# Half of a graph layer's rows turned by VectorE through DRAM, in a hand-made order, on one core

## Chip, cores, metric

The kernel runs on one core of one Trainium2 chip. The metric is the device time of one execution in microseconds (us). A ratio is the mean time of one kernel's fast runs over the mean of the other's in the same rounds on the same chip, so it is not quite the ratio of the medians quoted beside it. The profile shows one execution of each kernel.

## The reference

4096 nodes of 512 features go through two layers, each with a layer norm, a relu and a residual:

```python
h = relu(layernorm(x));  x = x + L0(h, adj, ptr, Wq, bq, Wk, bk, Wv, bv)   # attention in 32 graphs of 128 nodes
h = relu(layernorm(x));  x = x + L1(h, adj, W, a_origin, a_dst)            # graph attention, 8 heads of 64

# L1, per head: mx = h @ W[head];  logits[i, j] = s_i + t_j
# attn = softmax over j of logits where adj > 0;  out = attn @ mx
```

In L1 the term s_i falls out of the softmax, so a row j needs only e_j = exp(t_j) for each head and the products e_j * mx_j. The kernel prepares these for 32 tiles ("rows" below) of 128 nodes, then multiplies each of 32 masks (adj > 0) with all of them. The change is in the preparation, here called the **row stage**.

## The kernel before

One row of layer 1 is normalised (VectorE and GpSimd), turned so that features lie on partitions (TensorE, with a relu on the way out of PSUM, the memory that its results land in), projected (TensorE), weighed by e (VectorE), and split into a rounded part (ScalarE) and a rest (GpSimd):

```python
def norm(src, hn):
    stats = small.tile([P, 6], F32, name="stats")
    nc.vector.bn_stats(stats, src)
    mv = small.tile([P, 2], F32, name="mv")
    nc.vector.bn_aggr(mv, stats)
    ...                                                    # rstd on GpSimd: add, then pow
    nc.vector.tensor_scalar(hn, src, mv[:, 0:1], rstd, ALU.subtract, ALU.mult)

def relu_T(ps_pool, hn, dst):
    pt = ps_pool.tile([P, KC, P], F32, name="pt")
    for k in range(KC):
        nc.tensor.transpose(pt[:, k, :], hn[:, ts(k, P)], ident)
    nc.scalar.activation(dst, pt, AF.Relu)

def prepare(i, hT, part):
    pm = project1(ps_p, hT, w1x)                           # 2 x 4 matmuls into two PSUM banks
    e = sb2.tile([P, EW], F32, name="e")
    nc.gpsimd.memset(e[:, EC:], 1.0)
    nc.scalar.activation(e[:, ES:EC], pm[1][:, HW : HW + H], AF.Exp)
    nc.gpsimd.tensor_copy(e_all[:, i, :], e[:, ES:EC])
    weigh(e, pm)                                           # two multiplications of 256 columns on VectorE
    split(e, part)
    parts.append(part)
...
for i in range(n - 1, NT):                                 # the row stage; a scheduler orders each engine
    hT = nhT
    if i + 1 < NT:
        nhT = normed1(i + 1)
    prepare(i, hT, part_tile(lo if i < LO else hi, i))
...
for i in range(NT - 1):                                    # the aggregation
    tot = aggregate(sb3, ps_g, i, lambda j: parts[j])      # begins with load_mask: load, turn, widen
```

## Time and profile before

| | before |
|---|---|
| device time, median of 6 runs | 966.8 us (965.0 to 967.74) |
| profiled execution | 962.86 us, span 961.1, clock 0.999 |
| row stage (last attention product of layer 0 starts, to first aggregation product) | 361.88 to 465.60: 103.7 us |
| after the row stage | 465.60 to 961.1: 495.5 us |

The prediction below reads the main lines. Two more are needed for the row stage: the first is the line of TensorE's timeline where the row stage begins (start, duration, engine, line, operation, destination and sources, shape, count). The second is a group of the view by line and shape between 345 and 470 us (busy us and mean ns, then idle time ahead of the group and who ended it).

```profile
361.88 1.02 PE L501 MATMUL pp<-v,sT 128*128 128x512 f32 x2
```

```profile
L127 PE MATMUL pt<-ident,row 128*128 128x128 f32 x99 | 15.2, 276 | 6.2 <-DVE row L121 6.1
```

Apart from the 1.17 us ahead of the aggregation, TensorE's idle time in this stage stands ahead of the turnings (L127), which wait for VectorE's normalisation (L121).

### The profile page before, as it was taken

Reading aid. Unit: us, or ns where it says so; the run is one execution under the profiler, and the core shown is the slowest. Engines: PE = TensorE matmul, PEld = TensorE weight load, DVE = VectorE, ACT = ScalarE, POOL = GpSimd, SP = SyncE. Lnnn points to the kernel's source line nnn. Section 1 sums busy time; section 2 is a strip of 40 time slices with the busy share of each in tenths; the row PEclk is TensorE's granted clock in tenths of the full one; section 3 lists DMA queues with packets and bytes.
Section 4 is the critical chain, followed back from the end, with each engine's and each line's share of the span. In section 5 each row is a group of like instructions: output and inputs, shape, how many; then the busy total and the mean of one; then the engine's idle time right before and its main releaser. Section 6 shows DMA issues by size and latency. Waiting matters only on the chain.

```text
span 961.1 us, 13194 instructions
## 1 busy us (share of the span) xinstructions
PE 937.3 (98%) x5051; PEld 817.2 (85%) x5051; DVE 460.7 (48%) x983; ACT 260.7 (27%) x507; POOL 185.0 (19%) x344
## 2 busy tenths in 40 slices
PE   8999999989999998899999999999999999999997
PEld 5676677766677776788899999999999999999997
DVE  4678777776766348655142332424233242423322
ACT  5766676666762222333100000000000000000000
POOL 2221213222122115555110101001010100101010
PEclk9999999999999999999999999999999999999999
DMA  9999889898884124222012213132231212122111
GB/s 347 419 349 389 314 324 368 351 369 343 343 335 158 34 87 122 77 66 55 1 54 80 85 49 88 49 83 54 79 82 50 88 50 83 52 80 81 51 45 35
DMA packets 58180, 148.22 MB, mean 154 GB/s; under 512 B 6402, under 2 KB 23170, under 8 KB 49922
## 3 DMA queue, kind: packets, MB, share of 16 engines
q1 hardware_dynamic: 48178, 130.31, 39.0%
q10 hardware_dynamic: 9936, 17.05, 4.7%
q8 instruction: 40, 0.66, 0.3%
q14 instruction: 26, 0.21, 0.1%
HBM read 113.77 MB, written 33.55 MB: 153 GB/s over the span
## 4 chain that ended last, share of the span: by engine, by line
PE 89%; DVE 4%; DMA 2%; POOL 2%; ACT 2%; issue 1%; SPq 0%; ACTq 0%; DVEq 0%; POOLq 0%
PE pg L284 50%; PE pp L428 11%; PE pp L416 10%; PE pp L243 9%; PE pp L501 3%; PE pss L474 3%; PE pt L127 2%; DMA row<-x_d 1%; PE pl L284 1%; POOL part L231 1%; DMA xg<-x 1%; DVE a L136 1%; DVE row L121 1%; ACT junk L451 1%; POOL rstd L120 0%
## 5 line engine op out<-in xcount | busy, mean ns | idle before, releaser
L284 PE MATMUL pg<-part,at 128*128 128x348 f32 x3008 | 479.6, 322 | 1.2 <-DVE e L252 1.2
L284 PEld LDWEIGHTS pg<-part,at 128*128 128x128 f32 x3008 | 479.1, 188 | 1.6 <-issue 1.5
L277 DVE CAST at<-at 128x4096 fp32r<-128x4096 fp8e4 x32 | 74.0, 2313 | 312.2 <-PE pg L284 312.2
L298 ACT COPY tot<-pg 128x522 f32<-128x522 f32 x31 | 18.5, 598 | 455.8 <-PE pg L284 455.8
L451 ACT ACTIVATE junk<-a 128x2048 bf16<-128x2048 f32 (+15 forms) x92 | 124.4, 1353 | 47.1 <-DVE x L503 25.0
L243 PE MATMUL pp<-w1x,hT 128*128 128x256 f32 (+1 forms) x512 | 117.3, 383 | 0.0
L428 PE MATMUL pp<-wv,hT 128*128 128x512 f32 x256 | 114.9, 592 | 0.0
L416 PE MATMUL pp<-hT,m_sb 128*128 128x256 f32 x512 | 113.2, 379 | 0.0
L416 PEld LDWEIGHTS pp<-hT,m_sb 128*128 128x128 f32 x512 | 96.2, 190 | 12.8 <-issue 0.5
L243 PEld LDWEIGHTS pp<-w1x,hT 128*128 128x128 f32 x512 | 94.9, 190 | 13.3
L428 PEld LDWEIGHTS pp<-wv,hT 128*128 128x128 f32 x256 | 48.6, 190 | 60.7 <-issue 60.7
L136 DVE TENSOR_SCALAR a<-a 128x512 fp8e4<-128x512 f32 x256 | 98.1, 460 | 1.8 <-DMA a_d<-a 1.8
L609 POOL COPY den_all<-tot 128x1 f32<-128x1 f32 x31 | 5.7, 184 | 369.2 <-DVE tot L299 369.2
L128 ACT ACTIVATE hT<-pt 128x512 f32<-128x512 f32 x64 | 36.9, 597 | 67.7 <-PE pt L127 67.6
L613 POOL TENSOR_TENSOR tot<-tot,row 128x512 f32<-128x512 f32 x31 | 39.9, 1288 | 61.8 <-DVE tot L304 61.8
L231 POOL TENSOR_TENSOR part<-e,part 128x522 fp32r<-128x522 f32 x32 | 42.2, 1318 | 43.1 <-ACT part L230 35.5
L118 POOL TENSOR_SCALAR ve<-mv 128x1 f32<-128x1 f32 x64 | 18.6, 294 | 150.9 <-DVE mv L116 150.8
L252 DVE TENSOR_TENSOR e<-pp,e 128x256 f32<-128x256 f32 x64 | 26.4, 415 | 29.3 <-ACT e L379 26.0
L270 DVE STREAM_TRANSPOSE at<-mw 128x1024 f32<-128x1024 f32 x32 | 39.6, 1236 | 0.0
L120 POOL TENSOR_TENSOR rstd<-ve,neghalf 128x1 f32<-128x1 f32 x64 | 38.4, 602 | 4.4
L432 DVE TENSOR_TENSOR v<-pp,bv_sb 128x512 f32<-128x512 f32 x32 | 22.0, 688 | 33.9 <-PE pp L428 33.9
L420 ACT ACTIVATE gT<-pp,c_sb 128x256 f32<-128x256 f32 x64 | 29.7, 467 | 28.7 <-PE pp L416 28.3
(101 smaller groups left out, 608.0 us busy)
## 6 DMA issues: line engine op xcount, KB each, us to landing
a<-adj SPq DMA_DIRECT2D x64, 1024.0 KB, 12.9
a_d<-a SPq DMA_DIRECT2D x32, 512.0 KB, 10.2
row<-x_d SPq DMA_DIRECT2D x64, 256.0 KB, 3.4
mw<-a_d SPq DMA_DIRECT2D x128, 128.0 KB, 4.0
xg<-x SPq DMA_DIRECT2D x16, 512.0 KB, 4.6
x_d<-x ACTq DMA_DIRECT2D x32, 256.0 KB, 4.2
out<-tot ACTq DMA_DIRECT2D x31, 256.0 KB, 3.8
wkT_sb<-wkT SPq DMA_DIRECT2D x4, 256.0 KB, 5.0
```

Of the source, the lines that this page charges most:

```text
L120: nc.gpsimd.tensor_tensor(rstd, ve, neghalf, ALU.pow)
L128: nc.scalar.activation(dst, pt, AF.Relu)
L136: nc.vector.tensor_scalar(a8v[:, u], av[:, u], 0.0, None, ALU.is_gt, saturate=False)
L231: nc.gpsimd.tensor_sub(dst[:, :, 1, :], e3, dst[:, :, 0, :].bitcast(F32))
L243: nc.tensor.matmul(pm[g][:, :n], hT[:, k, :], w1x[:, k, g * HW : g * HW + n], start=(k == 0), stop=(k == KC - 1),)
L270: nc.vector.transpose(at8.rearrange("p c n b -> p (c n b)").bitcast(F32).rearrange("p (c u n) -> p c u n", c=NW, n=B), mw.rearrange("p u ( ...
L277: nc.vector.tensor_copy(at.rearrange("p (c b) q -> p c b q", b=BY), at8.rearrange("p c q b -> p c b q"))
L284: nc.tensor.matmul(pg[:, : 2 * CW1], at[:, j, :], part(j)[:, c].rearrange("p s w -> p (s w)"), start=(j == 0), stop=(j == NT - 1),)
L416: nc.tensor.matmul(pp[:, : G * P], m_sb[:, k, ts(m, P)], hT[:, k, :], start=(k == 0), stop=(k == KC - 1),)
L428: nc.tensor.matmul(pp, hT[:, k, ts(t, P)], wv[:, k, :], start=(k == 0), stop=(k == KC - 1))
L451: nc.scalar.activation(junk[:, c0:c1], a[:, c0:c1], AF.Exp, scale=2.0 * NEG, accum_out=sums[:, n : n + 1],)
L613: nc.gpsimd.tensor_add(num, num, row)
```

## The change

The intent: take the turning of rows 16 to 31 off TensorE. VectorE turns blocks of 32x32 instead; four rows together ("a block", 1 MB) are written to DRAM and read back so that the right blocks come to the right partitions. The nodes of the four rows come out mixed, and the masks and the fallback path follow the mixed order. Because VectorE then has more to do, ScalarE weighs four of the eight heads for rows 8 to 15. VectorE, ScalarE, GpSimd and the load queue no longer follow the scheduler but the order of the program, and the first mask is loaded and converted within it; the second mask and the checks come after the rows. The core of the diff (the fallback and the mixed mask order are cut):

```diff
+MIXED = NT // 2          # rows 16 to 31 are turned by VectorE
+AHEAD = 8
...
-            n = len(ahead)
-            nhT = ahead[-1]
-            for i in range(n - 1, NT):
-                hT = nhT
-                if i + 1 < NT:
-                    nhT = normed1(i + 1)
-                prepare(i, hT, part_tile(lo if i < LO else hi, i))
+            def turn(i):
+                c, b = divmod(i, BY)
+                if b == 0:
+                    blocks[c] = sb4.tile([P, P // B, KC, BY, B], F32, name="blocks")
+                nc.vector.transpose(
+                    blocks[c][:, :, :, b], rows[i].rearrange("p (k q f) -> p q k f", k=KC, f=B)
+                )
+                if b == BY - 1:
+                    nc.sync.dma_start(hT_d[c], blocks[c].rearrange("p q k b r -> p q (k b r)"))
...
+                for i in range(n, NT):
+                    far, near = i + AHEAD, i + 2
+                    ...                                     # loads of rows
+                    if MIXED < far <= NT:
+                        turn(far - 1)
+                    if far % BY == 1 and MIXED + BY < far <= NT + 1:
+                        move(far // BY - 1)                 # four reads of a block from DRAM
+                    ...                                     # first mask: words, turn, widening
+                    low()                                   # GpSimd's rest of row i - 2
+                    if far < NT:
+                        of[far] = moments(rows[far])
+                    if near < MIXED:
+                        of[near] = moments(rows[near])
+                    ...                                     # TensorE turning of row i + 1 < 16
+                    pm = project1(ps_p, hTs[i], w1x)
+                    if before:
+                        low = finish(*before, later=True)   # weigh and copy row i - 1
+                    if near < MIXED:
+                        norm(rows[near], rows[near], of[near])
+                    if far < NT:
+                        norm(rows[far], rows[far], of[far])
+                    e = weights(i, pm)                      # exp
+                    halves = (1, 0)
+                    if i < MIXED:
+                        halves = (0,)
+                        for h in range(H // 2, H):
+                            nc.scalar.mul(...)              # ScalarE weighs four heads
+                    before = (e, pm, part_tile(lo if i < LO else hi, i), halves)
+                    if far < NT:
+                        nc.scalar.activation(rows[far], rows[far], AF.Relu)
```

More of the change, by code (lines that the diff above doesn't have):

```diff
@@ L84 @@
     a_d = dram.tile([NT, P, N // BY], F32, name="a_d")
+    hT_d = dram.tile([NW, P, P // B, KC * P], F32, name="hT_d")
     x1_d = dram.tile([NT, P, D], F32, name="x1_d")
@@ L108, in load_adj, with moments @@
         return a
-    def norm(src, hn):
+    def moments(src):
         stats = small.tile([P, 6], F32, name="stats")
@@ L120, in norm @@
         nc.gpsimd.tensor_tensor(rstd, ve, neghalf, ALU.pow)
-        nc.vector.tensor_scalar(hn, src, mv[:, 0:1], rstd, ALU.subtract, ALU.mult)
+        return mv[:, 0:1], rstd
+    def norm(src, hn, of=None):
+        mean, rstd = of or moments(src)
+        nc.vector.tensor_scalar(hn, src, mean, rstd, ALU.subtract, ALU.mult)
     def relu_T(ps_pool, hn, dst):
@@ L133, in mask_bytes @@
         a8v = a8.rearrange("p (u c q b) -> p u c b q", c=NW, q=B, b=BY)[:, :, half]
-        av = a.rearrange("p (c b u q) -> p u c b q", c=NW // 2, b=BY, q=B)
+        order = ("p (c b u q) -> p u c b q", "p (c u b q) -> p u c b q")[h]
+        av = a.rearrange(order, c=NW // 2, b=BY, q=B)
         for u in range(P // B):
@@ L225, in fold, with split, low @@
         return m_sb, c_sb, u_sb, z_sb
-    def split(e, dst):
+    def split(e, dst, later=False):
         e3 = e.rearrange("p (c w) -> p c w", c=CB)
         nc.scalar.copy(dst[:, :, 0, :], e3)
-        nc.gpsimd.tensor_sub(dst[:, :, 1, :], e3, dst[:, :, 0, :].bitcast(F32))
+        def low():
+            nc.gpsimd.tensor_sub(dst[:, :, 1, :], e3, dst[:, :, 0, :].bitcast(F32))
+        if later:
+            return low
+        low()
     def load_row(pool, i):
@@ L247, in project1, with weigh @@
         return pm
-    def weigh(e, pm):
-        for g in (1, 0):
+    def weigh(e, pm, halves=(1, 0)):
+        for g in halves:
             nc.vector.tensor_tensor(
@@ L257, in weigh, with load_words @@
             )
-    def load_mask(sb, i):
+    def load_words(sb, i):
         mw = sb.tile([P, P // B, N // BY // (P // B)], F32, name="mw", bufs=1)
-        for q in (0, 1, 2, 3):
+        for q in range(P // B):
             nc.sync.dma_start(
@@ L268, in load_mask, with turn_words @@
             )
+        return mw
+    def turn_words(sb, mw):
         at8 = sb.tile([P, NW, P, BY], FP8, name="at8", bufs=1)
@@ L275, in load_mask, with widen @@
         )
-        at = sb.tile([P, NT, P], F32R, name="at")
+        return at8
+    def widen(at, at8, c0=0, c1=NW):
         nc.vector.tensor_copy(
-            at.rearrange("p (c b) q -> p c b q", b=BY), at8.rearrange("p c q b -> p c b q")
-        )
+            at[:, c0 * BY : c1 * BY].rearrange("p (c b) q -> p c b q", b=BY),
+            at8[:, c0:c1].rearrange("p c q b -> p c b q"),
+        )
+    def load_mask(sb, i, at):
+        widen(at, turn_words(sb, load_words(sb, i)))
         return at
@@ L287, in product, with aggregate @@
         )
-    def aggregate(sb, ps_g, i, part):
-        at = load_mask(sb, i)
+    def aggregate(sb, ps_g, at, part):
         pg = ps_g.tile([P, CB, 512], F32, name="pg")
@@ L306, in graphs_are_tiles @@
     def graphs_are_tiles(sb):
-        ptr_i = sb.tile([1, NPTR], I32, name="ptr_i", bufs=1)
+        ptr_i = sb.tile([1, NPTR], I32, name="ptr_i", tag="row3", bufs=1)
         nc.sync.dma_start(ptr_i, ptr)
@@ L373, in normed1, with weights @@
                 return hT
-            def prepare(i, hT, part):
-                pm = project1(ps_p, hT, w1x)
+            def weights(i, pm):
                 e = sb2.tile([P, EW], F32, name="e")
@@ L380, in prepare, with finish @@
                 nc.gpsimd.tensor_copy(e_all[:, i, :], e[:, ES:EC])
-                weigh(e, pm)
-                split(e, part)
+                return e
+            def finish(e, pm, part, halves=(1, 0), later=False):
+                weigh(e, pm, halves)
                 parts.append(part)
+                return split(e, part, later)
+            def prepare(i, hT, part):
+                pm = project1(ps_p, hT, w1x)
+                finish(weights(i, pm), pm, part)
             with (
+                tc.tile_pool(name="adj0", bufs=AB, side="right") as ap,
                 tc.tile_pool(name="w0", bufs=1, side="right") as wp,
-                tc.tile_pool(name="adj0", bufs=AB, side="right") as ap,
                 tc.tile_pool(name="sb0", bufs=2, side="right") as sb,
@@ L574 @@
             )
-            n = len(ahead)
-            nhT = ahead[-1]
-            for i in range(n - 1, NT):
-                hT = nhT
-                if i + 1 < NT:
-                    nhT = normed1(i + 1)
-                prepare(i, hT, part_tile(lo if i < LO else hi, i))
+            sb5 = prep.enter_context(tc.tile_pool(name="sb5p", bufs=2, reuse_waits="tile"))
+            begun = ExitStack()
+            sb4 = begun.enter_context(
+                tc.tile_pool(name="sb4p", bufs=2, side="right", reuse_waits="tile")
+            )
@@ new lines, with load @@
+            rows, of, blocks, hTs = {}, {}, {}, {}
+            def load(i):
+                if i < NT:
+                    name, bufs = ("rowm", 5) if i >= MIXED else ("rown", 3)
+                    rows[i] = sb4.tile([P, D], F32, name=name, bufs=bufs)
+                    nc.sync.dma_start(rows[i], x1_d[i])
+            def turn(i):
[4 more added lines that the diff above has]
+                    blocks[c][:, :, :, b], rows[i].rearrange("p (k q f) -> p q k f", k=KC, f=B)
+                )
+                if b == BY - 1:
+                    nc.sync.dma_start(hT_d[c], blocks[c].rearrange("p q k b r -> p q (k b r)"))
@@ new lines, in move @@
+            def move(c):
+                hT = sb5.tile([P, P // B, KC, P], F32, name="hT4")
+                for q in range(P // B):
+                    nc.sync.dma_start(
+                        hT[ts(q, B)].rearrange("p u k m -> p u (k m)"),
+                        hT_d[c, :, q].rearrange("(u f) w -> f u w", f=B),
+                    )
+                for u in range(BY):
+                    hTs[c * BY + u] = hT[:, u]
+            E = mybir.EngineType
+            with tc.manual_schedule(engines={E.DVE, E.Activation, E.Pool, E.SP}):
+                n = len(ahead) - 1
+                hTs[n] = ahead[n]
+                before = None
+                for i in (1, 2):
+                    load(n + i)
+                for i in range(MIXED, n + AHEAD + 2):
+                    load(i)
+                norm(rows[n + 1], rows[n + 1])
+                low = lambda: None
+                for i in range(n, NT):
+                    far, near = i + AHEAD, i + 2
+                    if near + 1 < MIXED:
+                        load(near + 1)
+                    load(far + 2)
+                    if MIXED < far <= NT:
+                        turn(far - 1)
+                    if far % BY == 1 and MIXED + BY < far <= NT + 1:
+                        move(far // BY - 1)
+                    if far == NT + 1:
+                        begun.close()
+                        sb3a = straight.enter_context(
+                            tc.tile_pool(name="sb3a", bufs=1, side="right", reuse_waits="tile")
+                        )
+                        ata = sb3a.tile([P, NT, P], F32R, name="ata")
+                        words = load_words(sb3a, 0)
+                    if i == NT - 4:
+                        at8 = turn_words(sb3a, words)
+                    if i in (NT - 3, NT - 2):
+                        half = (i - NT + 3) * NW // 2
+                        widen(ata, at8, half, half + NW // 2)
+                    low()
+                    if far < NT:
+                        of[far] = moments(rows[far])
+                    if near < MIXED:
+                        of[near] = moments(rows[near])
+                    if i + 1 < MIXED:
+                        hTs[i + 1] = sb2.tile([P, KC, P], F32, name="hT1")
+                        relu_T(ps_t, rows[i + 1], hTs[i + 1])
+                    pm = project1(ps_p, hTs[i], w1x)
[10 more added lines that the diff above has]
+                        for h in range(H // 2, H):
+                            nc.scalar.mul(
+                                e[:, ts(h, HD)], pm[1][:, ts(h - H // 2, HD)],
+                                e[:, ES + h : ES + h + 1],
+                            )
+                    before = (e, pm, part_tile(lo if i < LO else hi, i), halves)
+                    if far < NT:
+                        nc.scalar.activation(rows[far], rows[far], AF.Relu)
+                low()
+                finish(*before)
@@ L590, with mask_of @@
         nc.gpsimd.memset(held, 1.0)
+        atb = sb3.tile([P, NT, P], F32R, name="atb", bufs=1)
+        def mask_of(i):
+            return ata if i == 0 else load_mask(sb3a, i, (ata, atb)[i % 2])
         def hold(n, src, bound, op):
@@ L607 @@
             nc.sync.dma_start(row, x1_d[i])
-            tot = aggregate(sb3, ps_g, i, lambda j: parts[j])
+            tot = aggregate(sb3, ps_g, mask_of(i), lambda j: parts[j])
             nc.gpsimd.tensor_copy(den_all[:, i : i + 1], tot[:, ES : ES + 1])
@@ L629 @@
         nc.sync.dma_start(row, x1_d[i])
-        at = load_mask(sb3, i)
+        at = mask_of(i)
         ps_l = straight.enter_context(tc.tile_pool(name="ps_l3", bufs=2, space=PSUM))
@@ L862, with level_rows @@
                     tc.tile_pool(name="ps_m4", bufs=2, space=PSUM) as ps_m,
-                    tc.For_i(0, NT, 1) as i,
                 ):
-                    hT = sb.tile([P, KC, P], F32, name="hT1")
-                    row = load_row(sb, i)
-                    norm(row, row)
-                    relu_T(ps_t, row, hT)
-                    pm = project1(ps_m, hT, w1x)
-                    te = small.tile([P, H], F32, name="te")
-                    nc.vector.tensor_tensor(te, pm[1][:, HW : HW + H], shift, ALU.subtract)
-                    nc.vector.tensor_scalar(te, te, 0.0, None, ALU.min)
-                    e = sb.tile([P, EW], F32, name="e")
-                    nc.gpsimd.memset(e[:, EC:], 1.0)
-                    nc.scalar.activation(e[:, ES:EC], te, AF.Exp)
-                    weigh(e, pm)
-                    split(e, parts_e[:, ds(i, 1)].rearrange("p o c s w -> p (o c) s w"))
+                    def level_rows(i, row):
+                        hT = sb.tile([P, KC, P], F32, name="hT1")
+                        norm(row, row)
+                        relu_T(ps_t, row, hT)
+                        pm = project1(ps_m, hT, w1x)
+                        te = small.tile([P, H], F32, name="te")
+                        nc.vector.tensor_tensor(te, pm[1][:, HW : HW + H], shift, ALU.subtract)
+                        nc.vector.tensor_scalar(te, te, 0.0, None, ALU.min)
+                        e = sb.tile([P, EW], F32, name="e")
+                        nc.gpsimd.memset(e[:, EC:], 1.0)
+                        nc.scalar.activation(e[:, ES:EC], te, AF.Exp)
+                        weigh(e, pm)
+                        split(e, parts_e[:, ds(i, 1)].rearrange("p o c s w -> p (o c) s w"))
+                    with tc.For_i(0, MIXED, 1) as i:
+                        level_rows(i, load_row(sb, i))
+                    with tc.For_i(MIXED, NT, BY) as i:
+                        for u in range(BY):
+                            row = sb.tile([P, D], F32, name="row1")
+                            for b in range(BY):
+                                nc.sync.dma_start(
+                                    row[ts(b, B)],
+                                    x1_d[ds(i + b, 1), ts(u, B)].rearrange("o p d -> (o p) d"),
+                                )
+                            level_rows(i + u, row)
                 with (
@@ L884 @@
                     nc.sync.dma_start(sofar, out[ds(i * P, P), :])
-                    tot = aggregate(sb, ps_g, i, lambda j: parts_e[:, j])
+                    at = load_mask(sb, i, sb.tile([P, NT, P], F32R, name="at"))
+                    tot = aggregate(sb, ps_g, at, lambda j: parts_e[:, j])
                     alone = small.tile([P, 1], F32, name="alone")
```

## The prediction

> **What bounds the kernel now.** I read the page first: busy shares, the forty slices, the chain that ended last.
>
> ```profile
> PE 937.3 (98%) x5051; PEld 817.2 (85%) x5051; DVE 460.7 (48%) x983; ACT 260.7 (27%) x507; POOL 185.0 (19%) x344
> ...
> PE 89%; DVE 4%; DMA 2%; POOL 2%; ACT 2%; issue 1%; SPq 0%; ACTq 0%; DVEq 0%; POOLq 0%
> ```
>
> TensorE is busy for 98% of the span and is 89% of the chain. So only two things can shorten the kernel: fewer TensorE instructions, or closing the gaps in which it waits. The change touches nothing before about 345 us (TensorE's order is the same in both programs up to layer 0's tail) and nothing but the mask buffers after about 465 us. So I split 345 to 470 us by stretches; the columns are length, then busy time and instruction count of each engine.
>
> ```profile
> 345.00:394.00 49.00, 42.83 (x207) 34.09 (x206) 36.27 (x81) 11.97 (x30) 21.81 (x40) 1.00 0.31 92
> 394.00:461.00 67.00, 67.00 (x341) 58.28 (x340) 36.60 (x82) 21.93 (x51) 37.88 (x83) 1.00 0.22 59
> 461.00:470.00 9.00, 7.83 (x44) 7.08 (x43) 2.57 (x7) 1.43 (x3) 2.60 (x3) 1.00 0.01 2
> ```
>
> From 394 to 461 us TensorE has no gap at all: layer 1's rows follow each other every 3.945 us (starts 398.07, 402.01, 405.96). Before that it idles 49.00 - 42.83 = 6.2 us, after it 1.2 us: 7.4 us together. The timeline of TensorE shows where:
>
> ```profile
> 376.88 0.66 PE L127 MATMUL pt<-ident,row 128*128 128x128 f32 x4 [3.02 <-DVE row L121]
> 385.76 0.66 PE L127 MATMUL pt<-ident,row 128*128 128x128 f32 x4 [1.20 <-DVE row L121]
> 393.63 0.66 PE L127 MATMUL pt<-ident,row 128*128 128x128 f32 x4 [1.54 <-DVE row L121]
> 465.60 4.70 PE L284 MATMUL pg<-part,at 128*128 128x348 f32 x28 [1.17 <-DVE e L252]
> ```
>
> A row's turning waits for VectorE's normalisation, because the scheduler had put two masks' conversions and the checks on ptr ahead of it on VectorE. In the chain, one row is "PE pt L127 x4" of 0.44 us (the turning) and "PE pp L243 x16" of 3.51 us (the projection).
>
> **What the Trainium skill says.**
> - "TensorE: Matmul & The Clock Gate", section "Architectural detail: the array is 16× 32×32, not 1× 128×128": ScalarE and VectorE are strict FIFO. The trace agrees: the 3.02 us gap above is a normalisation behind a 2.26 us mask conversion. This matters for a hand-made order: each wait in it stops all that stands behind.
> - "VectorE: DVE Perf Modes", section "The three transpose paths": VectorE turns 32x32 blocks only. That is why the change needs DRAM and mixed rows. The trace has the mask's turn, 1236 ns for 1024 elements a partition, so I estimate 0.65 us for 512.
> - "SBUF — State Buffer", section "Who interferes with whom": VectorE in a two-port mode and GpSimd exclude each other for a whole instruction. The trace agrees: the normalisation takes 0.55 us, but 1.44 us at 395.70, where GpSimd's 1.23 us subtraction had begun at 395.63.
> - "DMA: Bandwidth & Descriptors", section "Anatomy of one DMA — SWDGE (gpsimd) path": about 2 us are fixed. Here the path is another one; a 256 KB row load lands after 3.4 us (page, DMA issues), which agrees in size.
>
> **The change part by part.** Layer 0 already prepares rows 0 to 7; 24 rows remain, 8 to 31.
> - Removed from TensorE: the turning of rows 16 to 31, 16 x 0.44 = 7.0 us, all on the path.
> - Moved: the second mask's conversion and the ptr checks go behind the rows. This takes away what caused the 6.2 us of gaps.
> - Added to VectorE: 16 turns x 0.65 = 10 us; taken from it, eight weighings (8 x 0.42 us). Added to ScalarE: for rows 8 to 15 four multiplications each, for rows 16 to 31 a relu of 0.60 us in place of one from PSUM. ScalarE costs 0.18 us at 8 columns and 0.60 at 512 by the rows for exp and relu, that is 0.17 + 0.00083 per column; a per-partition operand adds 0.1 (128 columns with one: 0.394). So I estimate 0.31 us for 64 columns, one every 0.22.
> - Added DMA: four blocks of 1 MB out and back. DMA traffic in this stretch is 59 to 92 GB/s, against 350 in layer 0. A 1 MB weight load took 6.8 to 7.5 us in layer 0's traffic, so I estimate 6 us out and 7 back with issuing. The order gives a block four rows of time, over 14 us: hidden, with little to spare for the first block.
>
> If nothing else bound: 7.0 + 7.4 = 14.4 us, or 952.6 us. I don't expect all of that, because the order closes a **loop between VectorE and ScalarE**. In step i of the order VectorE does: turn row i+7, statistics of row i+8 (and of row i+2 while that is under 16), weigh row i-1, normalise i+2, normalise i+8. ScalarE does: copy row i-1's part, exp of row i, four multiplications (i under 16), relu of row i+8. The next turn waits for that relu; the relu stands behind exp and multiplications; these stand behind the copy, which waits for the weighing, which stands behind the turn. One round, with spacings from the trace (statistics to aggregate 0.72, aggregate to next 0.10, VectorE to ScalarE 0.11, ScalarE to VectorE 0.03), counted from the last aggregate's end:
> - Steps 9 to 13: the copy starts at 0.45; exp at 1.2, because GpSimd clears its buffer only after two rows' reciprocal roots (0.06 + 0.31 + 0.57 after the second, then 0.15); multiplications 1.43 to 2.31; relu to 2.91; turn from 2.94; statistics 3.50, aggregate 4.22, again 4.32, 5.04 to 5.2. A round of **5.2 us**, against TensorE's 3.95.
> - Steps 14 to 16 lack one row's statistics (0.82): **4.3 us**.
> - Steps 17 on: no multiplications, two weighings to 0.67, copy 0.78, relu 1.63 to 2.23 (it waits for the normalisation at 1.52), turn 2.26, statistics 2.82, aggregate to 3.7: **3.7 us**, against TensorE's 3.51.
>
> TensorE cannot run away from it: row i+2 needs the PSUM that weighing row i frees, and the turning of row i+1 needs a normalisation that follows the weighing. Positions: row 8 starts about 363.2 us (363.78 before); its first half ends at 365.0, then exp, multiplications, relu 1.75, turn and statistics 2.2, weighing 0.42, so the weighing in step 9 ends near 369.4. Then 4 x 5.2 = 20.8, 3 x 4.3 = 12.9, 7 x 3.7 = 25.9: step 23's weighing at 429.0. Row 24 starts 0.35 earlier; from there no statistics are left and TensorE sets the pace: 8 x 3.51 = 28.1, so row 31 ends at 456.7, against 464.43 now. The wait before the aggregation I put at 0.6 instead of 1.17. First aggregation 457.3 instead of 465.60: a gain of 8.3 us. 966.96 - 8.3 = **958.7, say 958.5 us**.
>
> **The rivals.**
> - TensorE-bound throughout: 952.6 us. For it: every engine's sum per row is under 3.95 us (VectorE 3.8, ScalarE 3.1 in the densest steps), and rows are ready two steps ahead. Against it: the loop above is a latency, not a sum.
> - Collision on the shared port: if in steps 9 to 13 GpSimd's subtraction (1.23 us) begins before the second normalisation, relu comes 1.4 us later in each of five rounds: 7 us lost, about 965. For it: the margin I compute is 0.15 us. Against it: GpSimd's subtraction was put one step later, seemingly to avoid this.
> - The first block's round trip comes late: row 16 would wait for DRAM. Each us late costs at most one us; the slack is about 2 us, so I give it 0 to 3 us, once.
> - Layer 0's tail is delayed by six early row loads (1.5 MB, queued before the last pair's x): against it, that load waits in the queue until 304.26 us anyway and its rows are turned at 328.65.
>
> **Range and chances.** The floor is 952.6 us, since nothing else of TensorE's work shrinks and the aggregation (470 to 940 us, no gap) is the same work. Between floor and collision: 952 to 963.5 us. Faster by over 2% would need 19.3 us, more than the two sums hold: 0.03. Slower by over 2%: 0.02.
>
> **What would show it.** Right: row turnings from 256 to 192 of TensorE's instructions; the gaps of 3.02, 1.20 and 1.54 us gone; rows 11 to 15 spaced 4.3 to 5.2 us with TensorE waiting for VectorE, rows 18 to 23 near 3.7, rows 24 on 3.51; VectorE's turn waiting for ScalarE's relu; turn 0.65 us, multiplication 0.3 us. Wrong: rows at 3.95 and 3.51 without gaps (then the loop is not closed or shorter, and 952 holds); normalisations of 1.4 us in rows 9 to 13 (collision); row 16 waiting for a DMA. A change of the aggregation's pace would make the whole working wrong.

## The result and the profile after

After: 957.59 us median of 6 runs (956.98 to 958.84), against 966.8 of before; ratio 0.9908, 95% interval 0.9895 to 0.992. The prediction of 958.5 us with its range held. The profiled execution took 957.75 us, span 956.0, clock 0.998.

The page's busy line and its chain of work that ended last:

```profile
PE 934.7 (98%) x4987; PEld 810.8 (85%) x4987; DVE 465.0 (49%) x992; ACT 267.9 (28%) x539; POOL 179.9 (19%) x344
...
PE 86%; DVE 4%; DMA 4%; ACT 3%; issue 1%; POOL 1%; SPq 0%; ACTq 0%; DVEq 0%
```

TensorE has 64 instructions fewer (5051 to 4987: 16 rows by 4), and its share of the chain falls from 89% to 86%, while DMA and ScalarE gain. Something other than TensorE now sets a larger part of the end. The same stretches as in the prediction, same columns:

```profile
345.00:394.00 49.00, 47.18 (x223) 36.96 (x222) 28.46 (x67) 20.02 (x60) 24.68 (x52) 1.00 0.32 100
394.00:461.00 67.00, 64.35 (x285) 52.76 (x284) 38.79 (x81) 22.71 (x57) 36.86 (x76) 1.00 0.59 159
461.00:470.00 9.00, 9.00 (x59) 9.00 (x58) 5.89 (x11) 0.06 (x1) 2.48 (x1) 1.00 0.17 45
```

The idle 6.2 us of the first stretch are 1.8 now, but the middle one, which had no gap, has 2.65 us of them. TensorE's timeline shows what they are (the bracket is idle time ahead and who ended it):

```profile
364.31 1.02 PE L530 MATMUL pp<-v,sT 128*128 128x512 f32 x2
...
378.32 0.65 PE L136 MATMUL pt<-ident,rown 128*128 128x128 f32 x4 [0.89 <-DVE rown L130]
383.38 0.66 PE L136 MATMUL pt<-ident,rown 128*128 128x128 f32 x4 [0.44 <-DVE rown L130]
...
408.56 51.30 PE L259 MATMUL pp<-w1x,hT 128*128 128x264 f32 x224 [1.84 <-DVE e L268]
460.46 1.83 PE L308 MATMUL pg<-part,ata 128*128 128x348 f32 x10 [0.61 <-DVE e L268]
```

The turnings of rows 12 and 13 start 5.06 us apart, not 3.945, and wait for VectorE: TensorE follows the round of another engine. This is VectorE's timeline of one dense round (L623 turn, L118 and L120 statistics, L268 weighing, L130 normalisations):

```profile
379.42 0.71 DVE L623 STREAM_TRANSPOSE blocks<-rowm 128x512 f32<-128x512 f32 x1 [0.70 <-ACT rowm L698]
380.06 0.65 DVE L118 BATCH_NORM_STATS2 stats<-rowm 128x6 f32<-128x512 f32 x1
380.74 0.18 DVE L120 BATCH_NORM_AGGREGATE mv<-stats 128x2 f32<-128x6 f32 x1
380.84 0.66 DVE L118 BATCH_NORM_STATS2 stats<-rown 128x6 f32<-128x512 f32 x1
381.54 0.18 DVE L120 BATCH_NORM_AGGREGATE mv<-stats 128x2 f32<-128x6 f32 x1
381.64 0.39 DVE L268 TENSOR_TENSOR e<-pp,e 128x256 f32<-128x256 f32 x1
382.77 0.55 DVE L130 TENSOR_SCALAR rown<-rown,mv,rstd 128x512 f32<-128x512 f32 x1 [0.75 <-POOL e L400]
383.24 0.54 DVE L130 TENSOR_SCALAR rowm<-rowm,mv,rstd 128x512 f32<-128x512 f32 x1
384.48 0.71 DVE L623 STREAM_TRANSPOSE blocks<-rowm 128x512 f32<-128x512 f32 x1 [0.70 <-ACT rowm L698]
```

and ScalarE's of the same round:

```profile
382.14 0.63 ACT L240 CAST part<-e 128x522 fp32r<-128x522 f32 x1 [2.26 <-POOL ve L122]
382.67 0.17 ACT L401 ACTIVATE e<-pp 128x8 f32<-128x8 f32 x1
382.87 0.93 ACT L692 ACTIVATE e<-pp,e 128x64 f32<-128x64 f32 x4
383.81 0.63 ACT L698 ACTIVATE rowm<-rowm 128x512 f32<-128x512 f32 x1
```

This is the predicted loop. The weighing ends at 382.03; the copy (L240) starts at 382.14; exp, four multiplications and the relu (L698) follow without a gap; the relu ends at 384.44 and the next turn starts at 384.48. The profile puts the copy's wait down to GpSimd (L122, which ended at 382.08), only because that came last; the weighing had ended 0.05 us before it. The 16 turns start 5.05 us apart five times (the first of these 5.03), then 4.14 twice, then 3.74 eight times.

One wait in the row stage was not foreseen. VectorE's turn of the first mask stands ahead of a weighing and waits for its words (mw):

```profile
447.46 1.25 DVE L287 STREAM_TRANSPOSE at<-mw 128x1024 f32<-128x1024 f32 x1 [5.27 <-DMA mw<-a_d]
448.63 0.71 DVE L268 TENSOR_TENSOR e<-pp,e 128x256 f32<-128x256 f32 x2
```

The row stage runs from 364.31 to 460.46, 96.15 us: **7.6 us less** than before. What follows it takes 495.5 us in both. So the gain is all in the row stage as far as the profiles show it. The medians differ by 9.2 us; the profiled run of before was 3.9 us under its own median, so the two profiles alone can't place the rest.

### The profile page after: what moved, and what is told of

Its sections match the earlier page's. It is cut to its first block, busy times and chain, and to the rows that moved or that the text cites.

```text
span 956.0 us, 13142 instructions
## 1 busy us (share of the span) xinstructions
PE 934.7 (98%) x4987; PEld 810.8 (85%) x4987; DVE 465.0 (49%) x992; ACT 267.9 (28%) x539; POOL 179.9 (19%) x344
## 4 chain that ended last, share of the span: by engine, by line
PE 86%; DVE 4%; DMA 4%; ACT 3%; issue 1%; POOL 1%; SPq 0%; ACTq 0%; DVEq 0%
PE pg L308 50%; PE pp L457 12%; PE pp L445 10%; PE pp L259 5%; PE pp L530 3%; PE pss L503 3%; PE pt L136 1%; DMA row<-x_d 1%; DVE stats L118 1%; DMA a<-adj 1%; PE pl L308 1%; DVE blocks L623 1%; ACT rowm L698 1%; POOL rstd L124 1%; DMA mw<-a_d 1%
## 5 line engine op out<-in xcount | busy, mean ns | idle before, releaser
L308 PE MATMUL pg<-part,ata 128*128 128x348 f32 x1536 | 247.4, 322 | 0.6 <-DVE e L268 0.6
L308 PEld LDWEIGHTS pg<-part,ata 128*128 128x128 f32 x1536 | 245.0, 188 | 1.0 <-issue 1.0
L308 PE MATMUL pg<-part,atb 128*128 128x348 f32 x1472 | 237.3, 322 | 0.0
L308 PEld LDWEIGHTS pg<-part,atb 128*128 128x128 f32 x1472 | 235.0, 188 | 0.1
L296 DVE CAST atb<-at 128x4096 fp32r<-128x4096 fp8e4 x16 | 36.7, 2293 | 153.1 <-PE pg L308 153.1
L296 DVE CAST ata<-at 128x4096 fp32r<-128x4096 fp8e4 (+1 forms) x17 | 37.3, 2196 | 141.8 <-PE pg L308 141.8
L122 POOL TENSOR_SCALAR ve<-mv 128x1 f32<-128x1 f32 x64 | 16.3, 258 | 163.3 <-DVE mv L120 163.3
```

Of the source, the lines that this page charges most:

```text
L296: nc.vector.tensor_copy(at[:, c0 * BY : c1 * BY].rearrange("p (c b) q -> p c b q", b=BY), at8[:, c0:c1].rearrange("p c q b -> p c b q"),)
L308: nc.tensor.matmul(pg[:, : 2 * CW1], at[:, j, :], part(j)[:, c].rearrange("p s w -> p (s w)"), start=(j == 0), stop=(j == NT - 1),)
```

## The experiments

The question is where the rest of the 14.4 us went that the prediction had counted as possible. The theory: a loop between two engines that each work strictly in their order, closed because the turn stands at the head of VectorE's step. The rivals: TensorE or the sum of one engine's work sets the pace; the trip through DRAM; the mask's words. ("Turn" below is VectorE's turning of a row, L623.)

Each group of runs shared a chip with runs of before (medians 966.1, 966.19 and 965.78 us). "Row stage" is from the one profiled execution.

| run | median us (runs) | ratio to before, 95% | row stage us |
|---|---|---|---|
| e0_again | 957.32 (4) | 0.9908, 0.9894 to 0.9923 | 96.24 |
| e1_turn_mid | 951.92 (4) | 0.9856, 0.9841 to 0.9871 | 90.27 |
| e2_no_mul | 955.40 (4) | 0.9892, 0.9877 to 0.9906 | 94.40 |
| e3_all_tensor | 959.23 (6) | 0.9934, 0.9918 to 0.995 | 97.13 |
| e4_longer | 963.69 (6) | 0.9982, 0.9966 to 0.9998 | 102.28 |
| e5_words | 959.90 (6) | 0.9934, 0.9915 to 0.9952 | 97.81 |
| e6_both | 951.75 (5) | 0.9845, 0.9826 to 0.9865 | 90.23 |
| e7_turn_early | 951.27 (5) | 0.9843, 0.9828 to 0.9859 | 89.32 |
| e8_turn_alone | 950.74 (5) | 0.9845, 0.9828 to 0.9862 | 88.88 |
| e9_turn_no_mul | 950.20 (5) | 0.9838, 0.982 to 0.9857 | 90.31 |

**e0_again: the kernel after, once more.** No edit.

> The changed kernel once more, as the base for the other runs on this chip. Both theories: 957 to 958.5 us. Row stage (from the last attend matmul of layer 0 to the first aggregation matmul) 96 us, against 103.7 in the kernel before; rounds of the turn on VectorE 5.05 us in steps 10 to 14 and 3.74 in steps 17 to 24.

957.32 us, and the same rounds. The row stage repeats within 0.1 us.

**e1_turn_mid: open the loop by moving one instruction.** The turn goes from the head of VectorE's step to between weighing and normalising. Same instructions, same data.

```diff
-                    if MIXED < far <= NT:
-                        turn(far - 1)
...
                     if before:
                         low = finish(*before, later=True)
+                    if MIXED < far <= NT:
+                        turn(far - 1)
```

> The turn of row i+7 is moved from the head of VectorE's step to the place between weighing and normalising. Loop theory (turn waits for the relu that stands behind exp and multiplications): the relu then has most of a step's time, the round drops to 3.6 us or less of its own, TensorE sets the pace with 3.95 and 3.51 us a row; row stage 89 to 91 us, total 951.5 to 954 us. Rival 1 (VectorE's work per step with its waits for GpSimd is the bound, not the loop): no faster than 956.5 us. Rival 2 (the blocks' trip through DRAM becomes the bound, as its slack falls to about 1 us): TensorE waits for a DMA at rows 16, 20, 24 or 28, total 954 to 957 us.

951.92 us, 5.4 us under e0. TensorE's timeline of e1:

```profile
364.86 3.67 PE L259 MATMUL pp<-w1x,hT 128*128 128x264 f32 x16
...
368.81 3.67 PE L259 MATMUL pp<-w1x,hT 128*128 128x264 f32 x16
...
372.75 3.67 PE L259 MATMUL pp<-w1x,hT 128*128 128x264 f32 x16
...
424.94 28.29 PE L259 MATMUL pp<-w1x,hT 128*128 128x264 f32 x128 [0.81 <-DMA hT<-hT_d]
453.83 8.37 PE L308 MATMUL pg<-part,ata 128*128 128x348 f32 x51 [0.61 <-DVE e L268]
```

The rows start every 3.945 us and wait for nobody until row 24, which waits 0.81 us for its block. VectorE's work is unchanged, so no sum of work had set the pace: it was the place of the turn. Now that the rows go faster, the trip through DRAM shows. (It shows in e2 too, with 0.34 us at row 20.)

**e2_no_mul: ScalarE weighs nothing.** VectorE weighs all heads of all rows, turn at the head as in the kernel after.

```diff
-                    if i < MIXED:
-                        halves = (0,)
-                        for h in range(H // 2, H):
-                            nc.scalar.mul(...)
```

> ScalarE's four multiplications are undone, VectorE weighs all eight heads of rows 8 to 15 again. Loop theory: the relu waits for the second normalisation just as long as for the multiplications (both end near 378.8 us in the round that I read), so the round stays 5.05 us and the time stays within 1 us of the changed kernel. Rival (VectorE is the loaded engine and ScalarE's help is what makes the order fit): 8 x 0.33 us more on VectorE, 2 to 3 us slower than the changed kernel.

955.40 us: 1.9 us **faster** than e0, which neither expectation held ("within 1 us" and "slower"). The starts of VectorE's turns in e2:

```profile
367.43 0.71 DVE L623 STREAM_TRANSPOSE blocks<-rowm 128x512 f32<-128x512 f32 x1 [2.25 <-ACT rowm L691]
372.46 0.71 DVE L623 STREAM_TRANSPOSE blocks<-rowm 128x512 f32<-128x512 f32 x1 [0.70 <-ACT rowm L691]
377.51 0.71 DVE L623 STREAM_TRANSPOSE blocks<-rowm 128x512 f32<-128x512 f32 x1 [0.70 <-ACT rowm L691]
```

The dense rounds stay at 5.05 us, as the loop theory said they would. In the round of the kernel after shown above one sees why: the relu starts at 383.81, when two things have just ended, the multiplications (383.80) and the normalisation of its row (383.78). Taking one away leaves the other. The gain is elsewhere: the first turn comes 4.06 us after the row stage begins (363.37 to 367.43) instead of 5.03 (e0: 364.28 to 369.31), because nothing else held the first relu back but the multiplications, and the two rounds of 4.14 us become 3.74. 0.97 + 2 x 0.40 = 1.8 us of the 1.84 by which the row stage is shorter. So the part of the change meant to relieve VectorE costs about 1.9 us in this order.

**e3_all_tensor: the hand-made order and the early mask, but TensorE turns every row.**

```diff
-MIXED = NT // 2
+MIXED = NT
```

(with the mask order of one kind, and the statistics, normalisation and relu of row i + 8 only where VectorE turns; no block goes through DRAM. The edit also makes ScalarE weigh four heads of all 24 rows.)

> The hand-made order and the early mask stay, but TensorE turns all rows again: no blocks, no trip through DRAM, no mixed rows. Loop theory: without the loop TensorE runs at 3.945 us a row without gaps, 24 rows and the rest of the stage make 95.8 us, so the total is about the changed kernel's: 957 to 959 us; the 7.0 us that VectorE's turning takes from TensorE are given back by the loop. Rival (the gain comes from the turning on VectorE, the order is worth little): 962 to 966 us.

959.23 us. TensorE's timeline of e3, and VectorE's last weighing:

```profile
367.09 3.67 PE L259 MATMUL pp<-w1x,hT 128*128 128x264 f32 x16
371.03 3.67 PE L259 MATMUL pp<-w1x,hT 128*128 128x264 f32 x16
...
458.98 15.53 PE L308 MATMUL pg<-part,ata 128*128 128x348 f32 x96 [1.85 <-DVE e L268]
```

```profile
458.41 0.41 DVE L268 TENSOR_TENSOR e<-pp,e 128x256 f32<-128x256 f32 x1
```

Rows start every 3.945 us without a gap, and the row stage (361.85 to 458.98) is 97.13 us, which is 6.6 us less than before. So the order, with the second mask's conversion out of the way, gives most of the gain by itself; no run separates the two. What the new way of turning adds is 0.9 us by the row stage and 1.9 by the medians (e3's runs spread from 956.02 to 962.00), of the 7.0 us that it takes off TensorE. Even the 0.9 us is not the turning's own: in e3 the last weighing stands on VectorE behind checks (L719 and L720, 455.96 to 458.41), so the aggregation waits 1.85 us instead of e0's 0.61. Without these 1.24 us the row stage of e3 would be 95.9 us, by estimate, and e0's is 96.24. So the 7.0 us go back, most of them in the loop (opening it in e1 gave 6.0 us of row stage; the mask's words take 0.59, see e5).

**e4_longer: lengthen the loop on ScalarE.** Two copies into an unused tile ahead of each relu; the result is unchanged.

```diff
                     if far < NT:
+                        for _ in range(2):
+                            extra = small.tile([P, P], F32, name="extra", bufs=1)
+                            nc.scalar.copy(extra, ident)
                         nc.scalar.activation(rows[far], rows[far], AF.Relu)
```

> The kernel after, with two more ScalarE copies of 128 columns into an unused tile ahead of each of the 15 relus of steps 9 to 23 (and step 8's), about 0.25 us apart, so some 0.5 us more of ScalarE a row. ScalarE is far from full: 3.1 us of 5.05 in the dense rounds. Loop theory (the turn waits for the relu, which stands behind all that ScalarE has before it): nearly every round gets longer by what is added, the dense ones from 5.05 to about 5.5 us, the last ones from 3.74 to about 4.15; 15 rounds by 0.42 to 0.5 are 6 to 7.5 us, so 963 to 965 us in all. Rival (TensorE or the sum of an engine's work sets the pace): nothing changes, 957.3 within 0.5 us.

963.69 us, as the loop theory expected, though the rounds grew somewhat otherwise than by its figures: the dense ones to 5.44 (+0.39), but one of them to 5.98, those of 4.14 to 4.64 (+0.50), the last to 4.01 (+0.27), but the first of these stays at 3.74. ScalarE of e4, then VectorE's turn behind it:

```profile
390.45 0.64 ACT L700 COPY extra<-ident 128x128 f32<-128x128 f32 x2
391.00 0.62 ACT L701 ACTIVATE rowm<-rowm 128x512 f32<-128x512 f32 x1
```

```profile
391.66 0.71 DVE L623 STREAM_TRANSPOSE blocks<-rowm 128x512 f32<-128x512 f32 x1 [1.08 <-ACT rowm L701]
```

The turn's wait for the relu grows from 0.70 to 1.08 us. An engine that was busy for 40.2 of the 101 us between 360 and 461 (kernel after) is on the path with all that stands ahead of its relu. The rival of sums, no effect, falls.

The round of 5.98 us is the collision that the prediction had named as a rival. In that round alone GpSimd's subtraction begins ahead of VectorE's second normalisation (378.42 against 378.64), and the normalisation takes 1.45 us instead of 0.54:

```profile
378.64 1.45 DVE L130 TENSOR_SCALAR rowm<-rowm,mv,rstd 128x512 f32<-128x512 f32 x1
380.78 0.71 DVE L623 STREAM_TRANSPOSE blocks<-rowm 128x512 f32<-128x512 f32 x1 [0.69 <-ACT rowm L701]
```

In the kernel after the normalisation is first by 0.09 us (383.24 against 383.33), so it escapes this narrowly.

**e5_words: the mask's words ahead of the last block.** Their loads are issued before the reads of the last block instead of behind them.

```diff
-                    if far % BY == 1 and MIXED + BY < far <= NT + 1:
-                        move(far // BY - 1)
                     if far == NT + 1:
                         ...
                         words = load_words(sb3a, 0)
+                    if far % BY == 1 and MIXED + BY < far <= NT + 1:
+                        move(far // BY - 1)
```

> The kernel after, with the loads of the first mask's words issued ahead of the last block's reads instead of behind them. In the kernel after, VectorE's turn of the mask waits 5.27 us for these words, and the weighing of a row stands behind it; by the trace TensorE lost 0.9 to 1.0 us there. If that reading holds: 956.2 to 956.8 us and that gap is gone; the rounds of 5.05, 4.14 and 3.74 us stay. Rival (the wait was idle time of VectorE that cost nothing, or the block's reads become late in their turn): 957.3 within 0.4 us, or slower by up to 1 us with row 28 waiting for its block.

959.90 us: slower than the kernel after by 2.6 us of the medians on different chips (e0), 1.6 us of the row stage. The first reading fails; the rival named the wait that came, but put it at no more than 1 us. TensorE of e5:

```profile
447.97 14.26 PE L259 MATMUL pp<-w1x,hT 128*128 128x264 f32 x64 [2.05 <-DMA hT<-hT_d]
```

The mask's words did come earlier (their turn begins 77.8 us into the row stage, against 83.2), but the four reads of the last block are issued 1.8 us later (439.97 against 438.12 for the words that took their place), and row 28 waits 2.05 us. Issued first, the words still can't leave before the block's write has landed: in the trace of e5 their load waits 3.5 us for it. My reading of the cost was also too high: by the spacing of the exps the mask's words cost the kernel after 0.59 us (443.60 to 454.72 for three rows, 11.12, against 3 x 3.51), not 0.9 to 1.0.

**e6_both: e1 and e5 together.**

> The turn between weighing and normalising (as in e1_turn_mid), and the mask's words ahead of the last block's reads (as in e5_words). In e1 the mask's turn already waited only 3.05 us and TensorE showed no gap there, so the second edit should add next to nothing: 951.4 to 952.1 us. Were the two gains additive: 951.0. The 0.81 us wait of row 24 for its block stays, as the turn still stands behind the weighing.

951.75 us, row stage 90.23: e1 again. TensorE waits 0.46 us at row 24 and 0.43 at row 28 for the block, in place of e1's 0.81. (The profile puts the first of these down to a weighing, that of row 23, which row 24 doesn't need: the PSUM that it takes was freed by the weighing of row 22, which ended at 423.70, 3.5 us before. What is left is the block.)

**e7_turn_early and e8_turn_alone: a better place for the turn.** Between the statistics and the weighing; in e7 with the words early, in e8 with that move only.

```diff
-                    if MIXED < far <= NT:
-                        turn(far - 1)
...
                     pm = project1(ps_p, hTs[i], w1x)
+                    if MIXED < far <= NT:
+                        turn(far - 1)
                     if before:
                         low = finish(*before, later=True)
```

> The turn between the statistics and the weighing, and the mask's words early. Loop theory: the statistics no longer lie between the turn and the weighing; the dense round loses two statistics (5.05 - 1.65 = 3.4 us) and the late one loses one (3.74 - 0.79 = 2.95 us), both under TensorE's 3.95 and 3.51, so rows follow TensorE's pace as in e1. The turn does not wait for TensorE's projection, so the block's write leaves earlier than in e1, and row 24's wait of 0.81 us goes: 950.3 to 951.4 us. Rival (the block's trip through DRAM is late for another reason, its own length): as e1, 951.9 within 0.4 us, with a wait for the block still there. If the turn's wait for the relu still closes a loop through the weighing, rows are slower than 3.95 us and the time is over 953 us.

> The kernel after with one move only: the turn goes between the statistics and the weighing; the mask's words stay behind the last block's reads, where the kernel after has them. In e7 the words were issued early, and in e5 that edit alone did harm. Loop theory: the words' place is worth nothing once the loop is open, so this is e7 again: row stage 89.1 to 89.8 us, 950.6 to 951.7 us, no wait for a block. Rival (the early words did part of e7's work, as VectorE's turn of the mask holds up a weighing): slower than e7 by 0.5 to 1 us with a TensorE gap behind the mask's turn.

951.27 and 950.74 us, row stages 89.32 and 88.88. TensorE of e8:

```profile
361.85 1.02 PE L530 MATMUL pp<-v,sT 128*128 128x512 f32 x2
...
386.82 63.30 PE L259 MATMUL pp<-w1x,hT 128*128 128x264 f32 x288
450.73 1.51 PE L308 MATMUL pg<-part,ata 128*128 128x348 f32 x8 [0.61 <-DVE e L268]
```

Eighteen rows in one stretch, and 0.61 us ahead of the aggregation is all that TensorE waits. No wait for a block is left in e8 (e7 has 0.22 us at row 24): the third block's write leaves 47.9 us into the row stage (409.72), against 49.1 in e1 (412.61). About 0.6 us of this is the weighing that no longer stands ahead of the turn (411.24 to 411.88 in e1). The rest comes in through the loads: in both runs the statistics ahead of that turn wait for a row (2.65 us in e1, 2.22 in e8) whose load stands in the queue behind the second block's reads, and these were issued at 402.17 in e1, 38.6 us into the row stage, but at 399.31 in e8, 37.5 us. The early words are worth nothing here; VectorE's turn of the mask still waits 2.66 us in e8 and nobody is held up. This version beats both kernels: 15.0 us under before, by the medians of its rounds.

**e9_turn_no_mul: e8, and ScalarE weighs nothing.**

> As e8, and ScalarE's multiplications undone, so VectorE weighs all eight heads of rows 8 to 15. In the kernel after that edit gave 1.9 us, because the first relu came 1 us earlier and two rounds were shorter. Loop theory: with the loop open the relu is no longer what the next round waits for, and VectorE has 0.46 us of idle time per dense round (it waits for GpSimd before the first normalisation), which takes in the 0.33 us of the second weighing: equal to e8 within 0.4 us. Rival A (the multiplications relieve VectorE, which is the fuller engine now, 3.5 us of 3.95 in a dense round): slower than e8 by 0.3 us a row in five rows, 1 to 2 us. Rival B (the first relu still sets the first row): faster than e8 by 0.5 to 1 us.

950.20 us against 950.74, with runs from 948.51 to 951.97 and from 948.47 to 951.91: equal, as the loop theory expected; of the rivals, A (1 to 2 us slower) is not seen in the times, B (0.5 to 1 us faster) is at the edge of what these runs can tell. In its profile, the row stage is 1.4 us longer than e8's, with one wait of 1.21 us at row 24:

```profile
425.43 28.29 PE L259 MATMUL pp<-w1x,hT 128*128 128x264 f32 x128 [1.21 <-ACT part L240]
```

The copy that the line names (L240, that of row 23) is nothing that row 24 reads, and the weighing of row 22 had ended at 421.18. The block is left, and its reads were issued at 417.66, 6.2 us after its write at 411.43, against 4.5 us in e8 (409.72 to 414.23). The write itself left no later than in e8 (47.4 us into the row stage against 47.9), so it is the block's trip that was longer; one profile can't say whether that belongs to the edit. What is shown: with the loop open, the multiplications on ScalarE bring nothing that the times can see.

## Why the prediction was right

- **The bound and the removed work.** TensorE bound the row stage before; 64 turnings are gone, and so are the gaps of 3.02, 1.20 and 1.54 us. e3 and e8 show that both terms were real: the gaps give 6.6 us (e3, with its longer wait at the end), and with the turnings the row stage can fall by 14.8 us (e8), against the 14.4 of the prediction's floor, which was thus a little high. One reading was too simple: the normalisation behind the 3.02 us gap stood behind a mask conversion, as the prediction says, but it also waited 0.93 us for GpSimd and took 1.44 us instead of 0.55 (375.39).
- **The loop.** Its rounds were put at 5.2, 4.3 and 3.7 us; they are 5.05, 4.14 and 3.74. e1 opens it by the place of one instruction and gains 5.4 us; e4 lengthens it by a part that stands idle most of the time and loses 6.0 us of the row stage. That it is a latency and not a sum of work is shown.
- **The positions.** In the profile after, layer 0 ends 2.43 us later than in that of before (364.31 against 361.88). Less that, the weighing of step 9 ends at 369.5 (predicted 369.4), that of step 23 at 428.75 (429.0), the first aggregation starts at 458.0 (457.3).
- **A term missed.** Those last 0.7 us are the mask's words: the prediction had the mask's turn in no wait at all, and it cost 0.59 us. The row stage therefore gave 7.6 us and not 8.3. The turn took 0.71 us, not 0.65. That the total still came within 1 us of 958.5 is in part luck: the medians differ by 9.2 us, 1.6 more than the profiled row stages, and nothing in the prediction accounts for these.
- **A step with the right sum and a half-right reason.** The dense round was worked out with the multiplications on its path. In the trace they tie with the normalisation, so taking them off leaves the round as it is (e2); where the tie is absent, at the first row and in two rounds, they cost 1.8 us.
- **The rivals.** The collision didn't come to the loop of the kernel after: normalisations stay at 0.54 to 0.55 us in the dense rounds; GpSimd's subtraction pays instead (1.53 us in a dense round, against 1.23 in the late ones). But the order doesn't exclude it: the margin is 0.09 us, not the 0.15 of the prediction, and e4 has it in one round, at 0.54 us. No row of the kernel after waits for a block; when rows go faster, some do (0.81 us in e1), and when its reads stand behind the words, row 28 does (2.05 in e5). Layer 0 isn't delayed by the new loads: in e8, which has them, it ends at 361.85 us, as before.
- **Open.** Layer 0's end differs between profiles from 361.85 to 366.54 us, and goes with the mean granted clock (0.999 in before, e3 and e8; 0.995 in e6). Why the clock differs from run to run is not settled. Nor is the whole difference between the medians: in the profiles the row stage accounts for 7.6 of after's 9.2 us, and for all but 0.2 to 2.2 us of the other runs' differences (most in e9).

## What to carry to other kernels

When work is moved to another engine in a fixed order, look not at each engine's sum but at the round: an instruction that waits for another engine belongs as late in its step as its own reader allows, with all that doesn't need it ahead of it; here that one move was worth 7.4 us of the row stage (e0 to e8), more than the new way of turning had brought where it first stood. Try the order alone before the new mechanism, since the order, with the mask's work moved, gave 6.6 of 7.6 us. But keep the mechanism in mind when the order is better: with the turn in its good place the row stage fell by 14.8 us. A load queue has an order too: what is put ahead to help one reader is paid for by the next.

## What the Trainium skill lacked or had wrong

- No page describes a loop of waits closed by the order of two strict FIFO engines. "TensorE: Matmul & The Clock Gate" names the FIFO; the runs show its price: a round of 5.05 us in which VectorE was busy for 3.6 and TensorE needed 3.945, and 5.4 us of device time for the place of one instruction.
- "VectorE: DVE Perf Modes", section "The three transpose paths", has one size in its table, 128x128 in bf16 (390 ns for TensorE, 311 for VectorE). In fp32 VectorE's turn of 128x512 took 0.71 us and of 128x1024 1.24 us, while four pipelined 128x128 turnings took 0.44 us of TensorE's path, so per element TensorE was the faster one. The page doesn't say that the 32x32 blocks can be put together through DRAM, nor what that trip takes: in e8 3.9 to 4.8 us from the issue of a 1 MB write to that of the first read, and 5.1 us (median) more until a read lands.
- "DMA: Bandwidth & Descriptors", section "Anatomy of one DMA — SWDGE (gpsimd) path": its fit, 2.0 us + bytes / 436e3, gives 4.4 us for the block's write of 1 MB, which landed after 4.4 us on another path. For a read of 256 KB it gives 2.6 us; with four in flight together they took 5.4 (the fit's 4.4 us for their 1 MB as one transfer is nearer).
- "SBUF — State Buffer", section "Who interferes with whom", says that one side is blocked for the whole instruction of the other; it gives no size for a partial overlap. In the kernel after, GpSimd's subtraction began with 0.45 us of VectorE's normalisation to go and grew by 0.30 us (1.23 to 1.53), the normalisation by nothing; in e4's one round with the subtraction ahead, they overlapped by 1.16 us (378.64 to 379.80) and the normalisation grew by 0.91 (0.54 to 1.45). In both, the one that came second grew by somewhat less than the overlap; spans on GpSimd are rough, and no run shows in which mode VectorE's normalisation ran.
